# The soft-disc attention layer of a four-layer kernel: steps of a column of four blocks in place of steps of a pair of blocks

## The chip, the core and the metric

The kernel runs on one core of a Trainium2 chip. Its time is device microseconds of one execution, and a version's time is the median over its executions. A core has five engines with a queue of instructions each, worked off in order: TensorE (PE: matrix products, with weight loads of their own, PEld), VectorE (DVE), ScalarE (ACT: functions from tables), GpSimd (POOL) and SyncE (SP: it issues DMAs). [...] Products land in PSUM, which has eight banks of 128 x 512 float32 here.

## What is computed

Four layers work on x, 8 images of 32 x 32 tokens with 256 channels, float32; each adds its result to x after a group normalisation without weights. The first three (retention, an mLSTM, neighbourhood attention) are not touched. The fourth, cut to what matters:

```python
qkv = silu(x @ w_qkv.T)
q, k, v = split(qkv, 3)
q, k = rms_norm(q) * w_qn, rms_norm(k) * w_kn          # per head of 32, 8 heads
wp = silu(x @ w_wp.T + b_wp)
width = sigmoid(wp[..., :8]) * max_dist + 0.5
sharp = sigmoid(wp[..., 8:]) * 9.5 + 0.5
scores = q . k over a 7 x 7 window, * 32 ** -0.5
soft_mask = sigmoid((width - rel_dist) * sharp)
attn = softmax(scores - (1 - soft_mask) * 10000)
out = rms_norm(attn . v over the window) * w_on
x = x + silu((out + v) @ w_out.T)
```

(The reference also rotates q and k, by an angle that depends on the head alone; within a head it is the same for both and cancels in q . k, and the kernel leaves it out, before and after.)

## The kernel before, in words

`layer3` (from line 1991) treats an image's 32 x 32 tokens as a 4 x 4 grid of blocks of 8 x 8. A block's 64 queries see 14 x 14 = 196 keys. Heads come in halves c of four. A *pair* is two blocks under each other in one column (`disc_pairs`, line 1513): 128 queries on the 128 partitions, so an image half has 8 pairs, an image 16, the layer 128 (`st.groups`). For a pair n there are, in order:

- `soft(n)`: four tanh on ACT (line 2133, 128 x 196 each), the soft disc's mask, into one of nine probability tiles `e0` to `e8`; `masked(n)`: one addition on POOL (line 2140, 128 x 784) that shuts out what lies outside the window
- `scores(n)`: 16 products on PE (line 1706) into four PSUM banks, one a head; `logits(n)`: four reductions on DVE (line 1719) that add scores and mask in place and take the row's extremum
- `exps(n)`: four exponentials on ACT (line 1729), which also sum
- `divide(n)`: a reciprocal on DVE (line 1736) and a multiplication on POOL (line 1737)
- `turn(n, i)`: four transposes on PE (line 1747) and a copy on DVE (line 1752), for each i of two
- `values(n)`: products with v on PE (line 1763, 12 in the program, 24 in the trace) and two copies on DVE (line 1771).

All PSUM tiles (four of scores, two of `turn`, one of `values`, and those of the side work) come from one ring of eight banks.

Side work is cut into units that `Fillers` holds with a due time in steps; `units(at)` emits what is due. An image half J (`plan_chunk`) has six projections (`project`, line 2045: two products, a tanh on ACT, line 2042, and a `rest` on DVE and POOL), the sums of squares and their roots (`roots`, line 2144: a table load, a logarithm and an exponential on ACT), four spreading products with scalings of q and k (`head_scale`, line 2171), v laid out in strips on POOL (`in_strips`) and turned on PE (`vturn`). An image (`plan_image`) has its load, statistics, normalisation (`normed`, two on ACT), the disc's parameters (`discs`, line 2083), and its tail: `tail_sq`, `tail_scale`, `reload`, `output` (line 2223). What a unit leaves for DVE and POOL goes to `later`, and `finish()` emits it.

The four compute engines' order is written out by hand: the loop at the end of `layer3` (from line 2347) runs over pairs, and the order in which it calls these functions is the order in each queue. In step n it works on pair n+3 (scores, logits), n+1 (exponentials), n+5 (tanh, mask), n (division), n-2 (turn) and n-3 (values). Every eighth step is `rooted`: there the next half's roots are taken.

Of the kernel before, what the change touches and what calls it, by code (L numbers as in the profile page):

```python
# [1512 lines left out]
def disc_pairs():  # L1513
    return [
        Pair((r, r + 1), c, (8 * r, 8 * r + 8), 8 * c, 14, 14, 0)
        for c in range(4)
        for r in (0, 2)
    ]


# [154 lines left out]
class DiscStream(Stream):  # L1675

# [5 lines left out]
    def __init__(self, K, wk, cp, pp, pairs, n_img, ebufs):  # L1684
        super().__init__(K, wk, pp, pairs, n_img, ebufs)
        self.slots, self.s, self.su = 20, {}, {}
        shape = [P, 4, 2 * self.PART]
        self.tiles = [cp.tile(shape, F32, name=f"e{i}") for i in range(ebufs)]

# [6 lines left out]
    def prob(self, n):  # L1696
        return self.tile(n)[:, :, self.ROW : self.ROW + NWIN]

    def scores(self, n):
        b, c, t = self.groups[n]  # L1700
        s = [self.ring(f"s{j}") for j in range(4)]
        q, k = self.q[b, c], self.k[b, c]
        for g in range(2):
            for j in range(4):
                ch = slice(32 * j, 32 * j + 32)
                self.nc.tensor.matmul(
                    grid(s[j][64 * g : 64 * g + 64, :NWIN], self.ROW),
                    q[ch, 64 * t.block(g) : 64 * t.block(g) + 64],
                    k[ch, t.krs[g] : t.krs[g] + self.ROW, t.kc : t.kc + self.ROW],
                    start=True, stop=True,  # L1710
                )
        self.s[n] = s

    def logits(self, n):

        s, e = self.s.pop(n), self.prob(n)
        self.mx[n] = self.wk.tile([P, 4], F32, name="mx", bufs=self.ebufs)
        for j in range(4):
            self.nc.vector.tensor_tensor_reduce(  # L1719
                e[:, j], in0=s[j][:, :NWIN], in1=e[:, j], scale=MASK_SCALE,  # L1720
                scalar=3.0e38, op0=ALU.add, op1=ALU.min,
                accum_out=self.mx[n][:, j : j + 1],
            )

    def exps(self, n):
        mx, e = self.mx.pop(n), self.prob(n)
        su = self.su[n] = self.wk.tile([P, 4], F32, name="su", bufs=4)
        for j in range(4):
            self.nc.scalar.activation(  # L1729
                e[:, j], e[:, j], AF.Exp, scale=-1.0, bias=mx[:, j : j + 1],  # L1730
                accum_out=su[:, j : j + 1],
            )

    def divide(self, n):
        e, su = self.prob(n), self.su.pop(n)
        self.nc.vector.reciprocal(su, su)  # L1736
        self.nc.gpsimd.tensor_mul(e, e, su.unsqueeze(2).to_broadcast([P, 4, NWIN]))  # L1737

    def turn(self, n, i):

        if i == 0:
            self.pts[n] = self.wk.tile([P, 2, HALF], F32, name="pts", bufs=2)
        ps = self.ring("pt")
        for j in range(2):
            for k in range(2):
                at = (2 * j + k) * P
                self.nc.tensor.transpose(  # L1747
                    ps[: self.PART, at : at + P],
                    self.tile(n)[:, 2 * i + j, k * self.PART : (k + 1) * self.PART],
                    self.K.ident,  # L1750
                )
        self.nc.vector.tensor_copy(self.pts[n][: self.PART, i, :], ps[: self.PART, :])  # L1752

    def values(self, n):
        b, c, t = self.groups[n]
        pts = self.pts.pop(n)
        v, at = self.v[b, c], 5 * t.col + t.rows[0]
        o = self.ring("o")

        for k, q0, o0, w in ((1, 64, 0, P), (0, 0, 64, 64), (2, 192, 0, 64)):  # L1760
            for j in range(4):
                p0 = (j % 2) * 2 * P + q0
                self.nc.tensor.matmul(
                    o[32 * j : 32 * j + 32, o0 : o0 + w],
                    v[: self.PART, at + k, 32 * j : 32 * j + 32],
                    pts[: self.PART, j // 2, p0 : p0 + w],
                    start=k == 1, stop=k != 1, skip_group_check=True,
                )
        for g in range(2):
            d = self.o[b, c][:, t.token(g) : t.token(g) + 1]  # L1770
            self.nc.vector.tensor_copy(
                bass.AP(d.tensor, d.offset, [d.ap[0], [SIDE, 8], [1, 8]]),
                o[:, 64 - 64 * g : 128 - 64 * g].rearrange("p (i j) -> p i j", j=8),
            )
# [216 lines left out]
def layer3(tc, K, src, dst, n_img, a, first):  # L1991
    nc = tc.nc
    pairs = disc_pairs()
    with tc.tile_pool(name="l3c", bufs=1, reuse_waits="tile") as cp, tc.tile_pool(
# [9 lines left out]
        kpad = [cp.tile([P, PADW, PADW], F32, name=f"kp{i}") for i in range(3)]  # L2004
# [3 lines left out]
        st = DiscStream(K, wk, cp, pp, pairs, n_img, 9)  # L2008
        for i in range(3):
            st.clear(i)  # L2010
# [34 lines left out]
        def project(J, s, h):  # L2045
            b, c = divmod(J, 2)
            if h == 0:
                if s == 0:
                    st.q[b, c] = wk.tile([P, L], F32, name="qT", bufs=3)
                elif s == 1:  # L2050
                    st.k[b, c] = kpad[J % 3]
# [76 lines left out]
        def soft(n):  # L2128
            b, c, t = st.groups[n]
            i, e = pairs.index(t), st.prob(n)  # L2130
# [7 lines left out]
        def masked(n):  # L2138
            e = st.prob(n)
            nc.gpsimd.tensor_add(e, e, win[:, 1].unsqueeze(1).to_broadcast([P, 4, NWIN]))  # L2140

        def roots(J, b):
# [19 lines left out]
            n = P if heads else 64  # L2164
# [6 lines left out]
        def head_scale(J, s):  # L2171

            ps = [st.ring("fac_ps") for _ in range(2)]
            for h in range(2):
# [261 lines left out]
```

## Time and profile before

| | |
|---|---|
| median of 3 executions | 3210.92 us (3210.78 to 3218.26) |
| profiled execution | 3219.66 us |
| its span in the profile | 3217.9 us |
| busy, share of the span: PE, DVE, ACT, POOL | 96%, 70%, 68%, 56% |
| the stretch 2500 to 3187 us (soft-disc layer): PE, DVE, ACT, POOL busy | 657.6, 574.3, 580.6, 562.6 of 687 us |
| granted TensorE clock in that stretch | 0.95 |
| first and last reciprocal of line 1736 | 2496.4 and 3183.0 us |

The profile's page cuts the span into 40 slices and gives each engine's busy share in tenths; the last ten are the soft-disc layer. Groups of instructions are given by line, engine, operation and tiles, with their count, busy time, the mean of one and the idle time of the engine ahead of them with what ended it. The ends of PE's products are modelled, so its busy time is an upper bound of its work. The view of the chain that ended last gives nothing here: it holds only the last 5 us.

### The profile page before, as it was taken

To read this page: it belongs to the slowest core of one execution; us is meant where nothing else is said; L and a number is where in the kernel's file an instruction comes from. 1 tells how busy PE (TensorE), PEld (TensorE's weight loads), DVE (VectorE), ACT (ScalarE), POOL (GpSimd) and SP (SyncE) were. 2 spreads that over 40 slices of the span, in tenths; PEclk is the share of its full clock that TensorE was granted. 3 is DMA by queue.
4 is the path that set the end of the run, shared out by engine and by line. 5 is a ranking of instruction groups with operands and counts; after the bars stand their busy time and mean duration, and the time that the engine had idled before them with its cause. 6 is when DMAs were issued, how large, how long until landed. Compare 5 with 4: busy or idle time off the path is not lost. (4 is left out here: it accounts for less than half of the span.)

```text
span 3217.9 us, 76380 instructions
## 1 busy us (share of the span) xinstructions
PE 3096.7 (96%) x30248; PEld 1631.9 (51%) x30248; DVE 2248.8 (70%) x5649; ACT 2186.5 (68%) x4945; POOL 1800.8 (56%) x1201
## 2 busy tenths in 40 slices
PE   7999999999999899999999999999998999999997
PEld 3323223233232444677777766666665555555554
DVE  4786777777776577575666656666665888888885
ACT  3667767776676557655555537667676888888785
POOL 4666666666655111354544545343435778888787
PEclk9999999999999999999999999999998999999998
DMA  3000000000000566888787741111111001111001
GB/s 136 11 27 1 27 27 1 27 21 8 27 14 27 207 242 230 259 224 199 204 229 205 201 153 27 52 68 41 42 52 50 15 15 41 41 41 41 28 28 44
DMA packets 139462, 267.99 MB, mean 83 GB/s; under 512 B 9376, under 2 KB 77984, under 8 KB 130784
## 3 DMA queue, kind: packets, MB, share of 16 engines
q1 hardware_dynamic: 132720, 242.73, 24.7%
q10 hardware_dynamic: 6384, 20.37, 1.9%
q8 instruction: 239, 3.92, 0.5%
q14 instruction: 119, 0.97, 0.1%
HBM read 177.87 MB, written 85.20 MB: 82 GB/s over the span
## 5 line engine op out<-in xcount | busy, mean ns | idle before, releaser
L693 DVE TENSOR_TENSOR e<-s,ret 128x1024 f32<-128x1024 f32 x512 | 602.3, 1218 | 175.8 <-PE s L687 173.3
L700 ACT ACTIVATE ea<-e 128x1024 f32<-128x1024 f32 x512 | 535.4, 1055 | 259.7 <-DVE e L693 237.0
L702 POOL TENSOR_TENSOR ea<-ea 128x1024 f32<-128x1024 f32 x128 | 304.1, 2376 | 288.4 <-ACT ea L700 220.4
L1605 POOL TENSOR_TENSOR e<-e,su 128x616 f32<-128x616 f32 (+2 forms) x128 | 157.3, 1229 | 269.9 <-DVE su L1604 240.2
L687 PE MATMUL s<-qk,qk 32*128 32x512 f32 x2048 | 302.4, 642 | 4.0 <-POOL qk L570 1.8
L739 PE MATMUL num<-e,v 128*32 128x512 f32 x2048 | 272.3, 597 | 0.0
L2133 ACT ACTIVATE e<-win,disc 128x196 f32<-128x196 f32 x512 | 238.9, 540 | 0.2
L1752 DVE COPY pts<-pt 112x512 f32<-112x512 f32 x256 | 174.1, 681 | 86.1 <-PE pt L1747 84.2
L1737 POOL TENSOR_TENSOR e<-e,su 128x784 f32<-128x784 f32 x128 | 191.7, 1497 | 74.6 <-DVE su L1736 37.1
L869 PE MATMUL up_ps<-x,wup 128*128 128x512 f32 x512 | 227.4, 598 | 4.0 <-POOL x L237 3.2
L1729 ACT ACTIVATE e<-e,mx 128x196 f32<-128x196 f32 x512 | 226.8, 447 | 0.0
L2140 POOL TENSOR_TENSOR e<-e,win 128x784 f32<-128x784 f32 x128 | 204.8, 1600 | 26.0 <-ACT e L2133 18.0
L1600 ACT ACTIVATE e<-e,mx 128x154 f32<-128x154 f32 (+2 forms) x512 | 212.3, 426 | 0.0
L712 PE MATMUL sm<-ea,ones 128*32 128x512 f32 x1536 | 209.7, 607 | 1.6 <-POOL ea L702 1.6
L1291 POOL TENSOR_TENSOR decayed<-state,rb 128x520 f32<-128x520 f32 x48 | 50.8, 1057 | 277.9 <-DVE state L1321 161.4
L896 DVE SCALAR_TENSOR_TENSOR cv<-xm,par,cv 128x512 f32<-128x512 f32 x192 | 144.7, 754 | 78.8 <-ACT cv L891 74.2
L2057 PE MATMUL qkv_ps<-xq,w 128*128 128x512 f32 x384 | 195.1, 635 | 4.2 <-DVE v L1785 2.5
L687 PEld LDWEIGHTS s<-qk,qk 32*128 32x128 f32 x2048 | 84.9, 183 | 197.9 <-issue 88.3
L1837 PE MATMUL qkv_ps<-x,w 128*128 128x512 f32 x384 | 183.0, 614 | 1.6 <-POOL x L237 1.6
L1085 ACT ACTIVATE d<-d,cols 128x128 f32<-128x128 f32 x512 | 163.3, 392 | 13.5 <-POOL d L1076 12.9
L1719 DVE CUSTOM_DVE_ANT_0 e<-s,e 128x196 f32<-128x196 f32 x512 | 153.7, 357 | 12.9 <-POOL e L2140 11.2
L1747 PE MATMUL pt<-idg,e 128*112 128x128 f32 x1024 | 157.8, 285 | 4.4 <-POOL e L1737 2.1
(241 smaller groups left out, 6823.1 us busy)
## 6 DMA issues: line engine op xcount, KB each, us to landing
d<-l1rows SPq DMA_DIRECT2D x64, 512.0 KB
x<-x SPq DMA_DIRECT2D x25, 1024.0 KB
l1xm<-xm SPq DMA_DIRECT2D x16, 1024.0 KB
l1sz<-sz SPq DMA_DIRECT2D x16, 1024.0 KB
xv<-l1xm SPq DMA_DIRECT2D x32, 512.0 KB
l1xa<-xa SPq DMA_DIRECT2D x16, 1024.0 KB
xa<-l1xa SPq DMA_DIRECT2D x16, 1024.0 KB
rb<-l1rows SPq DMA_DIRECT2D x32, 512.0 KB
```

The lines of the kernel that those rows point to most:

```text
L687: nc.tensor.matmul(s[:, j % 2], qk[b, 1, c][g, kb * P : (kb + 1) * P], qk[b, 0, c][g, h * HALF : (h + 1) * HALF], start=True, stop=True,)
L693: nc.vector.tensor_mul(e[n, i], s, m)
L700: nc.scalar.activation(ea[n, i], e[n, i], AF.Abs)
L702: nc.gpsimd.tensor_add(ea[n, i], ea[n, i], ea.pop((n - 1, i)))
L712: nc.tensor.matmul(acc["sm"][g, :], ones, two[j // 2][:, j % 2, :], start=kb == 0 and k == 0, stop=kb == 4 and k == 2,)
L739: nc.tensor.matmul(acc["num"][g, :], v[b][:, kb, vc], e[n, j // 2][:, j % 2, :], start=kb == 0, stop=kb == 7,)
L869: nc.tensor.matmul(ps, wup[:, kc, m * P : (m + 1) * P], seg(s)[:, kc], start=kc == 0, stop=kc == 1,)
L1600: self.nc.scalar.activation(p[:, j], p[:, j], AF.Exp, scale=-1.0, bias=mx[:, j : j + 1], accum_out=su[:, j : j + 1],)
L1729: self.nc.scalar.activation(e[:, j], e[:, j], AF.Exp, scale=-1.0, bias=mx[:, j : j + 1], accum_out=su[:, j : j + 1],)
L2057: nc.tensor.matmul(ps, w[:, kc, o : o + P], xq[b][:, kc, h * HALF : (h + 1) * HALF], start=kc == 0, stop=kc == 1,)
L2133: nc.scalar.activation(e[:, j], win[:, 0], AF.Tanh, scale=disc[b][:, i, 8 + h : 9 + h], bias=disc[b][:, i, h : h + 1],)
L2140: nc.gpsimd.tensor_add(e, e, win[:, 1].unsqueeze(1).to_broadcast([P, 4, NWIN]))
```

## The change

Only `DiscStream` and `layer3` are changed. A step now works on a *column* of four blocks, two pairs under each other (g = 0, 1): 64 steps in place of 128.

- Probability tiles are 128 x 2 x 4 x 224, five in place of nine of half the size. A head's scores of both pairs share one bank.
- `logits` takes the heads in two halves, and the division stands between them; one reciprocal serves both pairs.
- `turn(n, j)` handles one head of the column, its four transposes written so that blocks of queries that use the same strip of v lie side by side; `values` has five groups of products in place of twice three, and one copy of 256 columns in place of four of 64.
- Scores run two steps ahead, tanh three, exponentials one, turn one behind and values two behind.
- In a step ACT has the first pair's tanh, the units due, the second pair's tanh, then the exponentials in two parts with units between them. POOL has division and mask ahead of what `finish` brings.
- `roots` is split: the sum of squares is a unit (`squares_sum`), the logarithm and the exponential come at the end of every fourth step, ahead of that step's exponentials.
- The two `head_scale` of a half become one `head_scales`.
- Of q three buffers become two, of the padded k three become two, of the output tile five become four.
- All due times are restated in columns and quarters of a step.

The diff, cut to its core:

```diff
+class DiscStream:
+        shape = [P, 2, 4, 2 * self.PART]
+    def logits(self, n, heads):
+        for j in heads:
+            for g in (1, 0):
+                e = self.prob(n, g)
+                self.nc.vector.tensor_tensor_reduce(
+                    e[:, j], in0=s[j][:, 256 * g : 256 * g + NWIN], in1=e[:, j],
...
+    def turn(self, n, j):
+        d = ps[: self.PART].rearrange("p (g r k x) -> p g k r x", g=2, r=2, k=2)
+        for g in range(2):
             for k in range(2):
                 self.nc.tensor.transpose(
+                    d[:, g, k],
+                    self.tile(n)[:, g, j, k * self.PART : (k + 1) * self.PART],
...
-        for k, q0, o0, w in ((1, 64, 0, P), (0, 0, 64, 64), (2, 192, 0, 64)):
+        for k, m0, o0, w in (
+            (1, 64, 0, P), (3, 320, P, P), (0, 0, 0, 64), (2, 192, 64, P), (4, 448, 192, 64)
+        ):
...
-        for g in range(2):
-            d = self.o[b, c][:, t.token(g) : t.token(g) + 1]
-            self.nc.vector.tensor_copy(
-                bass.AP(d.tensor, d.offset, [d.ap[0], [SIDE, 8], [1, 8]]),
-                o[:, 64 - 64 * g : 128 - 64 * g].rearrange("p (i j) -> p i j", j=8),
-            )
+        self.nc.vector.tensor_copy(
+            grid(self.o[b, c], SIDE)[:, :, 8 * col : 8 * col + 8],
+            o[:, 0:256].rearrange("p (i j) -> p i j", j=8),
+        )
...
-            n, (b, c) = 8 * J, divmod(J, 2)
+            n, (b, c) = 4 * J, divmod(J, 2)
-                fill.add(n - 12 + i / 2, lambda s=s, h=h: project(J, s, h))
-            for s in range(2):
-                fill.add(n - 5 - s, lambda s=s: head_scale(J, s))
-            fill.add(n - 8.5, lambda: project(J, 2, 0))
-            fill.add(n - 8, lambda: project(J, 2, 1))
-            fill.add(n - 6, lambda: in_strips(J))
+                fill.add(n - 6.75 + i // 2 + i % 2 / 4, lambda s=s, h=h: project(J, s, h))
+            fill.add(n - 2.75, lambda: head_scales(J))
+            for h in range(2):
+                fill.add(n - 4.5 + h / 2, lambda h=h: project(J, 2, h))
+            fill.add(n - 2.75, lambda: in_strips(J))
...
-                fill.add(8 * J - 8, lambda J=J, t=t: roots(J, t))
+                fill.add(4 * J - 4.25, lambda J=J, t=t: squares_sum(J, t))
...
-            for n in range(-4, N + 3):
-                if 0 <= n + 3 < N:
...
+            for m in range(-2, N + 2):
+                rooted = m % 4 == 0
+                if m + 2 < N:
+                    st.scores(m + 2)
+                if m + 3 < N:
+                    soft(m + 3, 0)
+                units(m)
+                if m + 2 < N:
+                    st.logits(m + 2, (0, 1))
+                if 0 <= m < N:
+                    st.divide(m)
+                if m + 2 < N:
+                    st.logits(m + 2, (2, 3))
+                if m + 3 < N:
+                    soft(m + 3, 1)
+                    for g in range(2):
+                        masked(m + 3, g)
+                for i in range(2):
+                    if 0 <= m - 1 < N:
+                        st.turn(m - 1, 2 * i)
+                        st.turn(m - 1, 2 * i + 1)
+                    finish()
+                    if not rooted and 0 <= m + 1 < N:
+                        st.exps(m + 1, i)
+                    units(m + 0.25 + i / 4)
+                finish()
                 if rooted:
+                    roots(m // 4 + 1)
+                    if 0 <= m + 1 < N:
+                        st.exps(m + 1, 0)
+                        st.exps(m + 1, 1)
+                if 0 <= m - 2 < N:
...
+                    st.values(m - 2)
+                units(m + 0.75)
```

## The prediction

> **What bounds the kernel now.** I looked first at the busy shares in 40 slices, to find the soft-disc layer (the last quarter, from 2443 us to the end at 3217.9), then at the start times of the reciprocal of line 1736, one a pair of blocks: image by image its first one stands at 2496.4, 2580.0, 2673.2, 2761.7, 2853.8, 2946.6, 3040.8 and 3126.3 us, so an image with all its side work takes 83.6 to 94.2 us. Two such images, engine by engine (us, busy, granted clock, DMA):
>
> ```profile
> 2678.60:2770.50 91.90, 89.85 (x1002) 51.44 (x1001) 78.23 (x286) 79.57 (x230) 76.50 (x56) 0.98 0.11 36
> 2770.50:2862.40 91.90, 88.54 (x953) 50.88 (x952) 76.84 (x277) 75.97 (x221) 74.94 (x56) 0.94 0.11 36
> ```
>
> The order is PE, weight loads, DVE, ACT, POOL. PE is within 2 to 3 us of full (its ends are modelled), the other three stand 12 to 17 us below the period. Who waits for whom between 2500 and 3187 us, in us, times, longest:
>
> ```profile
> DVE pts L1752 <- PE pt L1747: 84.2, 81, 2.5
> ACT th L2042 <- PE qkv_ps L2057: 69.1, 33, 6.2
> ...
> ACT th L2042 <- PE out_ps L2227: 29.3, 27, 2.3
> POOL e L1737 <- ACT fac L2168: 29.3, 6, 5.6
> POOL e L1737 <- DVE su L1736: 29.1, 20, 3.5
> ```
>
> ACT's idle time is 106 of 687 us, and 98 of it is two waits for PE: the tanh of a projection (L2042) that PE has not finished. DVE's largest wait is for PE too. So PE sets the pace in the steps that project, ACT in those that take roots or have no side work. What one image holds (form, count, busy us, mean ns, idle before):
>
> ```profile
> L2133 ACT ACTIVATE e<-win,disc 128x196 f32<-128x196 f32 x64 | 29.9, 540 | 0.0
> L1729 ACT ACTIVATE e<-e,mx 128x196 f32<-128x196 f32 x64 | 28.4, 447 | 0.0
> L1737 POOL TENSOR_TENSOR e<-e,su 128x784 f32<-128x784 f32 x16 | 23.9, 1497 | 8.7 <-ACT fac L2168 4.9 <-DVE su L1736 3.7
> L1752 DVE COPY pts<-pt 112x512 f32<-112x512 f32 x32 | 21.8, 682 | 12.7 <-PE pt L1747 12.4
> ...
> L1771 DVE COPY oT<-o 128x64 f32<-128x64 f32 x32 | 5.5, 215 | 0.0
> ```
>
> **A measure of the old order.** From the timeline of 2770 to 2862 us, from one start to the next, PE takes 0.52 us for a pair's scores, 0.44 for four transposes, 0.58 for a pair's values (2.0 a pair in all), 1.8 for a projection, 1.75 for an output product, 1.85 for two spreading products of the roots, 1.9 for half an image's disc product, 1.05 for a tail product, 0.45 for a turn of v, 0.9 for the squares' sum (2.7 with the tail's). ACT takes 1.77 for four tanh or four exponentials (3.55 a pair), 0.55 for a projection's tanh, 1.23 for a normed half, 1.28 for a table load, 0.6 each for logarithm and exponential of the roots. Put in the sixteen steps of an image where the code has them, that makes 82.2 us for PE and 76.1 for ACT. The larger of the two, step by step, is 6.6, 7.3, 3.85, 7.65, 5.6, 5.6, 3.55, 4.7, 6.6, 4.85, 3.85, 5.1, 6.65, 7.35, 4.65, 8.2: together 92.1 us, against 91.9 of the window. So the old loop behaves nearly as if no step could lend time to the next, and I use the same measure on the new one.
>
> **The change, part by part.** *Fewer instructions.* Four copies of 64 columns a column of blocks become one of 256: the four take 4 x 0.175 us from start to start (two show as 0.35 in the timeline), the one, between 0.175 at 64 and 0.68 at 512 columns, 0.39; 0.31 saved, 2.5 us an image. One reciprocal instead of two saves some 0.08, 0.7 an image. Both are on DVE, which idles 15 us an image; I count them at nothing, and 3.2 us an image where DVE turns out to bound. Value products go from 24 to 20 a column with the same columns streamed; between nothing and 4/24 of 1.16 us, 0 to 1.5 us an image on PE; I take 0.5, near the columns' answer. Banks of PSUM fall from 19.3 to 14.3 a column, so scores wait less for a bank; the waits of L1706 are under 2 us an image now, so nothing. Tanh, exponentials, divisions, masks, table loads and DMAs keep their number (division and mask 1.5 and 1.6 us each on POOL). Loads and reloads are issued at the same place of the stream to within half a column; POOL has waited 0.7 us in all for them, so nothing while SP has slack.
>
> *The tanh of a projection moves.* It stood right behind four exponentials; now it stands behind two groups of tanh and one of exponentials (5.3 us), the second one behind 7.1. This answers the 98 us of waits: 13 us an image.
>
> *Steps become lumpy.* Eight steps an image, in each PE's 4.0 us and ACT's 7.1 plus the side work of the new schedule (two spreading pairs, two projections and half a disc product in step 1; two projections, half a disc product and two turns of v in 2; one projection, two turns, the squares in 3; one projection and the roots in 4; spreading, projections and two tail products in 5; two projections and an output in 6; one projection and two outputs in 7; projection, output, normed halves, roots in 0):
> PE 8.0, 13.1, 10.4, 9.4, 6.2, 13.3, 10.5, 11.3 = 82.2; ACT 13.1, 9.7, 8.7, 7.9, 10.1, 9.5, 8.75, 8.75 = 76.5. The larger each time: 13.1, 13.1, 10.4, 9.4, 10.1, 13.3, 10.5, 11.3 = 91.2 us. By this measure the change gives 0.9 us an image: the heavy PE steps stand where ACT is light and the reverse, in both orders.
>
> *What is added.* The last projection, v's second half, comes first in steps 0 and 4, and its tanh stands behind one group of tanh only. By the changed program's listing its bank is that of a tile which DVE empties after ACT's last tanh of the step before: two half copies of 0.42 and in step 0 an output's 0.68. So PE starts it 0.8 to 1.5 us into ACT's step, ends at 2.6 to 3.3, and ACT needs it at 1.77: 0.8 to 1.5 us, and another 1.2 for the output behind it in step 0. DVE may be later than that: in step 5 four scalings of q and k (2.6), two tail scalings (3.0), statistics (1.5) and the projections stand behind 5.6 us of fixed work, 4 us more than ACT's step. Then the logits of step 6 are late by these 4 us, the banks of the second projection with them, and ACT waits 1 to 2 us in steps 6 and 7. In steps 2 and 3 the disc's three scalings do the same; there POOL is busy, and these small instructions stretch (ns, least, median, longest):
>
> ```profile
> L2124 DVE SCALAR_TENSOR_TENSOR disc<-disc x16: 192/1158/1509, 2460.4 to 3067.5; 128x32 f32<-128x32 f32 x16
> ```
>
> Behind them are v's copies, and behind those PE's next projection. In all 2 to 6 us of new waits an image; the old order has its like (the two longest waits for a projection are 4.1 and 4.3 us in the second window), but there they are in the 92.1. I take 3, nearer the lower end since the longer cover repays a part: 91.2 - 0.5 + 3 = 93.7, 1.8 more than 91.9. Over seven images with side work: 12.6. Before the first reciprocal the same tanh and exponentials stand in ACT's queue; nothing. At the end the last column needs one more division (1.5) and two more copies (1.4) than the last pair: 3. Sum: 15.6, say 16.
>
> *The clock.* In the second window PE twice ran at less than full clock:
>
> ```profile
> 2789.00:2799.00 10.00, 7.64 (x90) 5.34 (x92) 9.11 (x32) 5.89 (x19) 8.29 (x7) 0.83 0.01 2
> ...
> 2814.00:2824.00 10.00, 9.66 (x63) 4.61 (x61) 8.17 (x34) 5.74 (x22) 8.23 (x7) 0.66 0.01 2
> ```
>
> By the granted share 10 x 0.17 and 10 x 0.34 us of PE's work are lost, 5 us an image. I leave this as it is: by the sums above PE idles some 9 us an image in the new order too, in pieces of a microsecond or two. [...]
>
> **Rivals.** (1) *The longer cover wins.* If steps lend time to each other, PE alone is the bound: 82.2 - 0.5, the 5 of the clock, and 1 to 2 of gaps, 88 to 89 us an image; 3 to 4 less than now, seven times 25, less the end's 3: 3189, and down to 3175 if two of the clock's 5 us go as well. For it: all 98 us of ACT's waits are at the moved instruction, and its cover grows from 1.77 to 5.3 us and more. Against: the measure above says that it was not order inside a step. (2) *A wash*: new waits of 0 to 2 us, 91 to 92 us an image: 3205 to 3218. (3) *POOL becomes the bound* on the slower side: in step 5 it has 6.2 us of divisions and masks, 5.1 of tail adds, 2.1 of squares and 1.75 of strips, 15.2 against ACT's 9.5, and no slack until step 0; the masks of step 6 would then end 4 us into step 7 and the output's add, whose tile one of three th buffers is, behind them. It decides once POOL is over 5 us late, and costs 3 to 5 us more an image: 3250 to 3262. It is the upper end of the likeliest case.
>
> **How the numbers follow.** The times stand against the profiled execution's own 3219.66 us (span 3217.9 and 1.8 around it), which is 8.7 above the median of 3210.92; I put the difference on the median: 3210.9 + 15.6 = 3227. A change under 0.3% (9.6 us) can't be told from none. Chances: slower by waits of DVE and the lumps 0.42, by POOL 0.09 (0.51 slower); a wash 0.14; faster by cover 0.35. The likeliest one's own range is 3221 to 3262; with the others, 3175 to 3262.
>
> **What would show it.** Right, if the idle time of ACT moves from the waits for projections at the steps' ends to the first projection of steps 0 and 4, each 2 to 5 us, DVE's wait for transposes stays over 50 us, and an image takes 93 to 95 us. Wrong, if ACT's waits for L2042's successor fall below 50 us over the layer and an image takes under 90; or if the granted clock rises to 1.0 there. POOL's case shows as DVE's logits waiting for masks.

## The result, and the profile after

| | before | after |
|---|---|---|
| median of 8 executions each, us | 3210.09 (3193.61 to 3218.26) | 3231.07 (3227.61 to 3240.39) |
| ratio, after to before | | 1.0072, 95% interval 1.0052 to 1.0091 |
| span of the profiled execution, us | 3217.9 | 3229.5 |
| layer: first reciprocal at, us | 2496.4 | 2489.7 |
| seven images, from first to first reciprocal, us | 629.9 | 641.4 |
| from the last image's first reciprocal to the end, us | 91.6 | 98.5 |

The changed kernel is slower by 0.5 to 0.9%. The two profiled executions are 11.6 us apart, the medians 21: the profiled execution of before took 3219.66 us, 9.6 above its median, that of after 3231.35. So the traces can place 11.6 us, and they place them thus: 6.7 less up to the first reciprocal, 11.5 more in the seven images, 6.9 more from there to the end.

The first view is that of stretches, two whole images of the changed kernel (us; then PE, weight loads, DVE, ACT, POOL busy; granted clock, DMA):

```profile
2665.40:2758.30 92.90, 81.71 (x889) 50.48 (x888) 75.91 (x246) 76.41 (x222) 73.95 (x55) 0.94 0.11 34
2758.30:2851.60 93.30, 82.52 (x889) 50.68 (x888) 75.85 (x248) 76.52 (x222) 73.95 (x55) 0.95 0.12 36
```

Each engine's work is what it was or less, PE's by 6 to 7 us (its ends are modelled, so that a part of this is no work), and an image takes 1 to 1.4 us longer. Who waits for whom between 2500 and 3187 us (in us, times, longest):

```profile
POOL e L1740 <- DVE su L1737: 106.8, 40, 6.7
...
DVE pts L1757 <- PE pt L1752: 58.9, 21, 8.6
ACT th L2044 <- PE qkv_ps L2059: 44.5, 25, 2.8
DVE su L1737 <- ACT e L1730: 41.7, 14, 5.3
...
ACT disc L2117 <- DVE disc L2112: 24.0, 7, 3.8
...
ACT th L2044 <- PE out_ps L2236: 19.7, 17, 1.6
```

ACT's waits for projections and outputs fell from 98 to 64 us. New ones came: the reciprocal waits for the exponentials, ACT for DVE's small operations on the disc, and POOL waits most of all, so over the whole stretch it is not the bound. The second image step by step, each step from its reciprocal to the next (same columns):

```profile
2758.30:2772.40 14.10, 10.24 (x114) 6.19 (x112) 7.34 (x30) 11.46 (x27) 7.29 (x5) 0.87 0.57 173
2772.40:2786.80 14.40, 13.15 (x115) 8.77 (x116) 8.96 (x30) 11.50 (x34) 9.83 (x8) 0.77 0.01 4
2786.80:2799.10 12.30, 10.51 (x130) 7.91 (x129) 12.27 (x32) 12.03 (x41) 11.70 (x9) 1.00 0.01 3
2799.10:2808.50 9.40, 8.95 (x104) 4.17 (x103) 9.37 (x33) 4.27 (x14) 6.01 (x4) 1.00 0.01 2
2808.50:2817.30 8.80, 7.97 (x109) 5.62 (x107) 7.73 (x31) 8.54 (x25) 6.01 (x4) 1.00 0.01 2
2817.30:2831.60 14.30, 11.70 (x104) 5.76 (x104) 12.86 (x38) 14.29 (x42) 13.18 (x11) 1.00 0.00 0
2831.60:2840.80 9.20, 9.20 (x110) 6.14 (x109) 8.81 (x34) 6.91 (x20) 9.20 (x8) 1.00 0.01 3
2840.80:2851.60 10.80, 10.80 (x113) 6.10 (x112) 8.52 (x32) 7.53 (x25) 10.72 (x9) 1.00 0.21 68
```

This is the table that the rest rests on. Look in each row for an engine whose busy time is the length of the step: from step 2 on there is one in every row: DVE in steps 2 and 3, ACT in 4 (nearly) and 5, PE in 6 and 7, where POOL is full as well. Only steps 0 and 1, the two behind the roots, have slack on every engine (11.46 of 14.10 and 13.15 of 14.40), and PE's 13.15 there is at a granted clock of 0.77. Over the whole image no engine is above 82.5 of 93.3 us; in its own step one of them nearly always is full.

Two cautions belong to this table. The first: busy is not the same as at work. In steps 2 and 3 DVE is held up inside small operations on the disc's parameters. In step 2 of the image that begins at 2665.4 us there are five (start, us, engine, line):

```profile
2695.04 1.39 DVE L2112 SCALAR_TENSOR_TENSOR disc<-dth,disc 128x64 f32<-128x64 f32 x1
...
2698.15 0.21 DVE L2099 TENSOR_TENSOR disc<-wp_ps,bwp 128x64 f32<-128x64 f32 x1
...
2698.88 0.41 DVE L2124 TENSOR_SCALAR disc<-disc 128x32 f32<-128x32 f32 x1
...
2699.21 1.62 DVE L2125 TENSOR_SCALAR disc<-disc 128x32 f32<-128x32 f32 x1
...
2700.86 1.50 DVE L2126 SCALAR_TENSOR_TENSOR disc<-disc 128x32 f32<-128x32 f32 x1
```

They take 5.1 us; the shortest that each of them takes in the traces of the changed kernel and of e2_disc adds up to 1.0 us. So DVE was occupied throughout the step, with some 8 us of work in 12.3. The second: a row is cut at DVE's reciprocals, and ACT's queue does not keep to them. A column alone has 24 ACT instructions (8 tanh, 8 exponentials, 8 reads of their sums); row 3 shows 14 in all, row 5 shows 42. So a row can be set beside the program's sum for that step only roughly.

### The profile page after: what moved, and what is told of

Read it like the earlier page. It is cut to its first block, busy times and chain, and to the rows that moved or that the text cites. A ratio compares the mean times of both kernels' runs of the same rounds, so it can differ in the third digit from the quotient of the medians.

```text
span 3229.5 us, 74992 instructions
## 1 busy us (share of the span) xinstructions
PE 3046.0 (94%) x29736; PEld 1626.0 (50%) x29736; DVE 2239.0 (69%) x5393; ACT 2187.6 (68%) x4945; POOL 1792.5 (56%) x1196
## 5 line engine op out<-in xcount | busy, mean ns | idle before, releaser
L2059 PE MATMUL qkv_ps<-xq,w 128*128 128x512 f32 x384 | 204.3, 661 | 37.1 <-DVE mx L1719 21.9
L1757 DVE COPY pts<-pt 112x512 f32<-112x512 f32 x256 | 163.1, 683 | 66.4 <-PE pt L1752 66.2
L1752 PE MATMUL pt<-idg,e 128*112 128x128 f32 x1024 | 143.2, 281 | 26.2 <-DVE qT L2069 10.7
L1719 DVE CUSTOM_DVE_ANT_0 e<-s,e 128x196 f32<-128x196 f32 x512 | 150.8, 351 | 20.7 <-PE s L1703 10.1
```

The lines of the kernel that those rows point to most:

```text
L2059: nc.tensor.matmul(ps, w[:, kc, o : o + P], xq[b][:, kc, h * HALF : (h + 1) * HALF], start=kc == 0, stop=kc == 1,)
```

## The experiments

Each kernel is an edit of the changed kernel or of one that stands above it. The ratio is to the kernel before, run beside each of them (its medians lie between 3207.9 and 3213.0 us), with the 95% interval. "Seven images" and "end" are the two stretches of the table above, from one profiled execution each; e3_v1 and e6_drain, alike up to the end, agree in them to 0.1 us an image, e8_lump and e10_best to 1.7, and the start (2487 to 2494 us in all these kernels) differs by 1 to 3 us in both pairs.

| kernel | edit | median, us | ratio | seven images | end |
|---|---|---|---|---|---|
| after | | 3231.07 | 1.0072 (1.0052 to 1.0091) | 641.4 | 98.5 |
| e1_recip | reciprocal behind all logits | 3228.45 | 1.0071 (1.0054 to 1.0089) | 640.4 | 99.8 |
| e2_disc | disc's functions later | 3229.68 | 1.0084 (1.0065 to 1.0103) | 641.2 | 98.5 |
| e3_v1 | v's second projection later | 3219.45 | 1.0043 (1.0030 to 1.0056) | 629.2 | 100.2 |
| e4_k0 | k's first projection ahead of the spreading | 3236.34 | 1.0091 (1.0077 to 1.0106) | 647.7 | 99.3 |
| e6_drain | e3, tail of image 6 later | 3215.63 | 1.0015 (1.0003 to 1.0027) | 629.1 | 95.2 |
| e7_cover | kernel before, tanh ahead of the units | 3221.41 | 1.0030 (1.0019 to 1.0041) | 641.2 | 88.3 |
| e8_lump | e3, two projections a step earlier | 3201.16 | 0.9971 (0.9958 to 0.9984) | 610.5 | 97.8 |
| e9_waits | e1 + e2 + e3 | 3230.10 | 1.0068 (1.0049 to 1.0087) | 632.5 | 98.7 |
| e10_best | e8 + e6's edit | 3196.57 | 0.9956 (0.9941 to 0.9970) | 609.4 | 93.4 |
| e11_disc2 | e10 + e2's edit | 3196.13 | 0.9954 (0.9940 to 0.9968) | 608.9 | 95.0 |
| e12_pool | after, division and mask behind the leftovers | 3350.86 | 1.0434 (1.0415 to 1.0453) | 760.7 | 98.7 |
| e13_recip2 | e10 + e1's edit | 3203.32 | 0.9972 (0.9960 to 0.9984) | 613.5 | 95.5 |

The steps of an image (mean of the five images from the second to the sixth, us from reciprocal to reciprocal), worked out from the same traces; before, such an image took 92.2 us:

| step | 0 | 1 | 2 | 3 | 4 | 5 | 6 | 7 | sum |
|---|---|---|---|---|---|---|---|---|---|
| prediction's sums | 13.1 | 13.1 | 10.4 | 9.4 | 10.1 | 13.3 | 10.5 | 11.3 | 91.2 |
| after | 13.7 | 13.9 | 12.3 | 9.5 | 9.1 | 14.6 | 9.5 | 10.8 | 93.4 |
| e1_recip | 12.5 | 12.7 | 12.2 | 10.2 | 8.6 | 15.0 | 9.6 | 10.8 | 91.7 |
| e2_disc | 13.7 | 13.7 | 10.8 | 10.2 | 9.5 | 15.4 | 9.5 | 10.8 | 93.6 |
| e3_v1 | 12.1 | 13.9 | 12.3 | 9.4 | 8.1 | 14.7 | 10.9 | 10.9 | 92.2 |
| e4_k0 | 13.7 | 13.8 | 11.4 | 9.3 | 8.9 | 15.8 | 10.2 | 10.8 | 93.9 |
| e8_lump | 12.1 | 12.2 | 12.6 | 9.3 | 9.2 | 12.8 | 9.8 | 10.5 | 88.6 |
| e9_waits | 11.0 | 12.7 | 10.4 | 10.3 | 9.4 | 17.3 | 9.9 | 10.9 | 91.8 |
| e10_best | 12.1 | 12.1 | 12.7 | 9.4 | 9.3 | 12.8 | 9.7 | 10.6 | 88.6 |
| e13_recip2 | 11.0 | 10.3 | 13.4 | 10.3 | 9.2 | 12.8 | 10.9 | 10.8 | 88.6 |

### Four waits taken away, one at a time

**e1_recip**

```diff
-                    st.logits(m + 2, (0, 1))
+                    st.logits(m + 2, (0, 1, 2, 3))
                 if 0 <= m < N:
                     st.divide(m)
-                if m + 2 < N:
-                    st.logits(m + 2, (2, 3))
```

> Edit of the changed kernel: all eight logits of a column stand ahead of its reciprocal, where four stood behind it. Theory A (the slow-down is made of waits that the new order makes; here DVE holds the banks of two heads while it waits for ACT's exponentials, 5.3 us of wait in the step after the roots, once in four steps, and the wait of DVE's reciprocal for ACT's exponentials is 41.7 us in all): the PE wait for the banks (2.1 us a time, two an image) goes, 13 to 22 us less than the changed kernel's 3231, so 3209 to 3218. Rival (the wait is hidden, or POOL, which now gets its division later, passes the delay on): within 10 us of 3231, or slower, with the wait of POOL's division for the reciprocal growing from 106.8 us.

The wait fell (41.7 to 24.3 us), POOL's wait for the reciprocal grew (106.8 to 122.7), and the ratio is that of the changed kernel, the last two as the rival said. But the steps did not give everything back: steps 0 and 1 are 1.1 and 1.2 us shorter, step 3 is 0.7 and step 5 0.4 longer, and each of the five middle images keeps 1.7 us. What takes these 8.7 us away again in the trace stands elsewhere: the first of the seven images and the last are each 4 us longer (87.0 and 95.2 against 82.9 and 91.5) and the end 1.3; the first reciprocal comes 2.6 earlier. In the last image it is step 5, which takes 18.3 us, 12.7 of them with PE at half clock (13.5 us and no half clock in the changed kernel). The steps with slack became shorter, as theory A said, and the kernel did not; why the first image became longer was not tried.

**e2_disc**

```diff
             def silu2(th):
...
-                return sigmoid
+                return lambda: sigmoid
```

(and the same one function earlier, for `silu`)

> Edit of the changed kernel: the two later functions that ACT takes for the disc's parameters (a silu and a sigmoid, both by tanh) are put off by one turn of the list of leftovers, so that they stand behind the next group of exponentials and not ahead of it. Theory A: the waits of ACT for DVE's small disc operations (24.0 + 8.0 us between 2500 and 3187, longest 3.8) go from ACT, and 10 to 25 us of the 32 from the time: 3206 to 3221. Rival (PE is the bound in those steps and lends the time away): the waits go and the time stays within 5 us of 3231, while the waits of ACT for projections grow by as much.

The rival, in every point that it named. Between 2500 and 3187 us:

```profile
ACT th L2044 <- PE qkv_ps L2059: 80.5, 35, 5.4
```

ACT's waits for the disc are gone, those for projections are 36 us longer (44.5 before the edit). In the table, step 2 becomes 1.5 us shorter, and steps 3, 4 and 5 take back 0.7, 0.4 and 0.8. DVE's hold-up moved with the edit: its operations on the disc took 5.1, 2.6 and 0 us in steps 2, 3 and 4 (mean of the five images), and now take 0.7, 3.5 and 1.9. So a DVE without slack in step 2 cannot be why the time stayed: it is now busy there for 8.1 of 10.8 us. What the hold-up itself costs was not tried apart.

**e3_v1**

```diff
-                fill.add(n - 4.5 + h / 2, lambda h=h: project(J, 2, h))
+                fill.add(n - 4.5 + h * 0.75, lambda h=h: project(J, 2, h))
...
-                fill.add(n + (14.5, 15.25, 15.5, 16)[i], lambda h=h, m=m: output(b, m, h))
+                fill.add(n + (14.5, 15.25, 15.5, 16.25)[i], lambda h=h, m=m: output(b, m, h))
```

> Edit of the changed kernel: the second projection of v stands a quarter of a step later (behind the second tanh group and the first exponentials of steps 0 and 4, not first in them), and the last output a quarter later too. This is the step of the prediction that takes 0.8 to 1.5 us of ACT wait in steps 0 and 4 and 1.2 for the output behind it. Theory A (as the prediction): the tanh's waits at the head of steps 0 and 4 (2.7 + 1.1 and 1.9 us in one image) go, 20 to 35 us less than 3231: 3196 to 3211. Rival (these steps are bound by PE, and the later place only moves the wait): within 10 us of 3231.

Steps 0 and 4 are 1.6 and 1.0 us shorter, step 6 1.3 longer; all seven images together 12.2 us. That is the whole excess of the changed kernel in the images: 629.2 against 629.9 before. By the ratios it is 0.0029 of 3210, 9 us: less than the theory's 20, and by the medians (11.6 us) just more than the rival's 10, so it falls between the two. It is the only one of the four edits that pays, and it acts in step 0, where no engine was full. It moves two things, v's projection and the last output, which were not tried apart.

**e4_k0**

```diff
-                fill.add(n - 6.75 + i // 2 + i % 2 / 4, lambda s=s, h=h: project(J, s, h))
+                fill.add(n - 6.75 - 0.01 * (i == 0) + i // 2 + i % 2 / 4, lambda s=s, h=h: project(J, s, h))
```

> Edit of the changed kernel: in the step after the roots the first projection of k is emitted ahead of the four spreading products and scalings, not behind them. Theory A: PE has a projection to do while it waits for the roots (the wait of PE and of its weight loads for the roots' factors, 14.5 and 16.0 us over six visible times, 2.4 to 2.7 us each) and does not fall to half clock behind it (10.2 us at half clock in one place, 92 us in the layer): 10 to 20 us less than 3231, with less time at half clock. Rival (the wait is that of the roots themselves on ACT, and the scalings then come later to scores that need them): within 10 us or slower, with the half clock as before.

The rival, on its slower side: step 1 keeps its 13.8 us, step 5 grows by 1.2. PE's wait for the roots fell from 14.5 to 4.2 us, but its wait for DVE's logits, which stood ahead of the projections (21.9 us), now stands ahead of the spreading products (21.8), and the half clock cost 40.0 us where it had cost 42.2. Filling the wait with work of the same step gained nothing.

### Two theories of a step's length

What remains is between two readings: that the position of an instruction inside its step matters (rival 1 of the prediction and my theory A), or that each step has its own load, and only moving load between steps helps (the prediction's measure).

**e7_cover** (edit of the kernel before)

```diff
-                if rooted and 1 < n + 5 < N:
+                if 1 < n + 5 < N:
                     soft(n + 5)
                 units(n)
...
-                if not rooted and 1 < n + 5 < N:
-                    soft(n + 5)
```

> Edit of the kernel before: the four tanh of the soft disc stand ahead of the step's units in every step, not only in every eighth, and nothing else changes (steps of a pair, divisions and masks as they were). This is the part of the change that the prediction's first rival lives by. Rival (the longer cover wins): the 98 us of ACT's waits for projections and outputs fall under 50 and the time by 10 to 25 us: 3185 to 3200. The prediction's measure (each step costs the larger of PE's and ACT's work, and the order inside it is worth little): waits fall, the time stays within 10 us of 3208.

It is slower by 0.3% (9.6 us by the ratio, just inside the 10 us of the prediction's measure) and 11.3 us longer in the seven images. Neither side was right about the waits between 2500 and 3187 us:

```profile
ACT th L2042 <- PE qkv_ps L2057: 78.4, 46, 6.2
...
ACT th L2042 <- PE out_ps L2227: 17.3, 20, 1.5
```

They are 96 us against 98: a cover of 3.5 us in place of 1.8 does not take the waits away, it moves them. (That the four tanh are missing behind the first projection, where the next one's tanh now waits, is my reading; it was not tried apart.) The images grow by 11.3 us here and by 11.5 in the whole change. So the earlier tanh alone costs, in the old order, all that the images lost, and e3_v1 wins as much back by moving v's projection and an output: which of the two parts is the cause in the new order is not shown.

**e8_lump** (e3_v1, and this)

```diff
-                fill.add(n - 6.75 + i // 2 + i % 2 / 4, lambda s=s, h=h: project(J, s, h))
+                fill.add(n - 6.75 + i // 2 + i % 2 / 4 - (0.5 + i / 4) * (i < 2 and J > 2), lambda s=s, h=h: project(J, s, h))
```

> Edit of the kernel e3_v1: the first two projections of each half (from the third on) stand at the end of the step before, where ACT is the longer engine by the prediction's sums (13.1 against PE's 8.0 us in step 0, 10.1 against 6.2 in step 4), and no longer in steps 1 and 5, where PE is (13.1 and 13.3 us). By the prediction's measure steps 1 and 5 lose 3.6 us each, steps 0 and 4 gain 1.1 each: 5 us an image, six images, 30 us: 3189, and the steps after the roots shrink from 13.9 and 14.7 us to about 11. Rival (steps lend each other time, so that PE's work counts wherever it stands): within 8 us of 3219.

Faster than the kernel before. Steps 1 and 5 become 1.7 and 1.9 us shorter (3.6 expected), step 6 another 1.1, step 0 stays and step 4 grows by 1.1: 3.7 an image, 18.7 over the seven, where 30 were worked out. The first two rows of an image of e3_v1, then the first, second and sixth of one of e8_lump:

```profile
2756.80:2769.10 12.30, 9.30 (x108) 5.61 (x106) 7.30 (x30) 9.60 (x24) 7.28 (x5) 0.97 0.57 171
2769.10:2783.20 14.10, 12.88 (x115) 8.51 (x116) 8.98 (x30) 11.51 (x33) 9.86 (x8) 0.79 0.07 21
```

```profile
2750.50:2762.80 12.30, 12.30 (x112) 6.83 (x110) 7.41 (x30) 9.59 (x24) 8.08 (x6) 1.00 0.62 185
2762.80:2774.90 12.10, 9.70 (x111) 7.58 (x111) 9.11 (x32) 11.05 (x32) 10.53 (x9) 0.86 0.10 31
...
2806.00:2818.80 12.80, 10.90 (x103) 6.42 (x102) 12.77 (x40) 12.79 (x40) 12.43 (x11) 0.87 0.00 1
```

In step 0 of e3_v1 PE had 9.30 of 12.30 us, and now it has 12.30 of 12.30. Step 5 does not come down to 11, which fits that DVE and ACT are busy throughout it and POOL nearly so. A projection moved within its step (e4_k0) was worth nothing; two moved over the step's border are worth 23 us by the ratios (0.0072 of 3210).

### Do the waits count once the load is levelled?

**e9_waits** (e1, e2 and e3 together) and, on the levelled kernel, **e11_disc2** (e10 with e2's edit) and **e13_recip2** (e10 with e1's):

> Edit of the kernel e3_v1 with the two edits of e1_recip and e2_disc, which gave 3 and 1 us alone. Theory (the waits that they remove were hidden because another engine came last in the same steps, and still does): within 5 us of 3219. Rival (v's projection was what hid them, so that now they count): 10 to 25 us less, 3194 to 3209.

> e10_best with the edit of e2_disc (disc's second and third functions behind the next exponentials). With the projections moved, step 2 is among the longest that are left (12.6 us from reciprocal to reciprocal, against 10.4 of PE's work by the prediction's sums). Theory (what is won in one step is given back in the next ones, in waits of ACT for projections and in time at half clock, as in e2_disc and e9_waits): within 5 us of e10_best. Rival (with the load levelled, ACT's waits for the disc are on the path now): 8 to 15 us less, step 2 at about 11 us.

> e10_best with the edit of e1_recip (all eight logits ahead of the reciprocal). In e1_recip steps 0 and 1 became 1.1 and 1.2 us shorter and step 3 and the last image longer, and the time stayed. Theory (given back elsewhere, as in e1_recip, e9_waits and e11_disc2): within 5 us of 3196.6. Rival (steps 0 and 1, 12.1 us each, are now among the longest and nothing takes the gain back): 7 to 16 us less, 3181 to 3190.

None gained. e9_waits is 8 us slower than e3_v1 by the ratios (their intervals touch), which neither side expected. In its trace steps 0 to 2 become 4.2 us shorter, steps 3, 4 and 5 take back 4.8, 2.6 of it in step 5, and step 6 is 1.0 shorter. So the five middle images keep 0.4 us each; the first image is 4.4 longer. The execution profiled is the fastest of six (3222.31 us), so the trace does not hold the 8 us. e11_disc2 is e10_best's equal. In e13_recip2 steps 0 and 1 become 2.8 us shorter, steps 2, 3 and 6 together 2.7 longer, and the sum is 88.6 for both. Its median is 7 us worse (5 by the ratios, whose intervals overlap); in the trace that is the first image, 4.1 us longer as in e1_recip and e9_waits, and 2 us each at the start and the end. PE had less time at half clock in it, too: 24.6 us of its work lost in 687, by the stretches for which the profile records a halved clock, against 35.8 in e10_best. That did not make it faster.

So the measure does not hold step by step: e13_recip2 has 11.0 us between the marks of step 0, where the prediction's sum for ACT is 13.1, so a part of that step's work stands beyond its marks. What the runs support is weaker: load moved between steps shortened the middle images more (3.7 us each, e8_lump) than any edit of the order inside steps (1.7 at most, e1_recip).

### The end, and GpSimd's order

**e6_drain** (e3_v1, and this; `b == n_img - 2` is image 6)

```diff
-                fill.add(n + 13.25 + c / 4, lambda c=c: tail_scale(2 * b + 4, b, c))
+                fill.add(n + 13.25 + 3 * (b == n_img - 2) + c / 4, lambda c=c: tail_scale(2 * b + 4, b, c))
...
+                late = (3.75, 3.25, 4.5, 4)[i] if b == n_img - 2 else 0
-                fill.add(n + (14.5, 15.25, 15.5, 16.25)[i], lambda h=h, m=m: output(b, m, h))
+                fill.add(n + (14.5, 15.25, 15.5, 16.25)[i] + late, lambda h=h, m=m: output(b, m, h))
```

(the last reload of that image moves with them)

> Edit of the kernel e3_v1 (v's second projection later): the scalings and additions of image 6's tail, and its outputs, are moved by three to four steps, behind the last two divisions. Theory: the 8.5 us that the changed kernel takes longer from its last reciprocal to the end (43.4 against 34.9; e3_v1: 46.1) are the five us of POOL's tail additions that stand ahead of the last two divisions, and what follows from them; with them behind, 5 to 9 us less than e3_v1's 3219, so 3210 to 3214, and no slower than before. Rival (the end is bound by PE, or by the squares and roots of the last image): within 3 us of e3_v1.

What it acts on stands in the timeline of the changed kernel (start, us, engine, line):

```profile
3180.59 4.99 POOL L2228 TENSOR_TENSOR oT<-oT,vT 128x512 f32<-128x512 f32 x4 [1.12 <-DVE oT L2225]
...
3182.74 0.20 DVE L1737 RECIPROCAL su<-su 128x8 f32<-128x8 f32 x1
...
3185.53 2.95 POOL L1740 TENSOR_TENSOR e<-e,su 128x784 f32<-128x784 f32 x2
...
3186.12 0.20 DVE L1737 RECIPROCAL su<-su 128x8 f32<-128x8 f32 x1
...
3188.43 1.28 POOL L2245 TENSOR_TENSOR xr<-xr,th 128x512 f32<-128x512 f32 x1
...
3189.66 2.95 POOL L1740 TENSOR_TENSOR e<-e,su 128x784 f32<-128x784 f32 x2
```

The division of the last column but one waits 2.8 us behind image 6's tail additions (its reciprocal is at 3182.74); that of the last one starts 3.5 us after its reciprocal, behind this division and an output's addition. With the tail behind them the end is 5.0 us shorter than e3_v1's (95.2 against 100.2), the ratio falls by 0.0028, 9 us, the upper end of what was expected. The other two forecasts were just missed: the median of 3215.63 stands above 3210 to 3214 (the kernel before took 3211.91 beside it, and 3207.90 beside e3_v1), and the kernel is still 0.15% slower than before, with an interval of 0.03 to 0.27%.

**e10_best** (e8_lump with e6's edit)

> The edits of e8_lump and e6_drain together on the changed kernel. They touch different stretches (the steps after the roots; what follows the last division), so they should add: e8_lump's 3201 less the 4 to 9 us that e6_drain gained on e3_v1: 3192 to 3197, faster than both kernels. If the two are not independent (the tail of image 6 is cover for PE in the last image), 3201 or more.

As expected, and faster than both kernels: 0.44% under the kernel before. Of the 5 us by which its median is under e8_lump's the intervals leave open whether it is 0 or 10.

**e12_pool**: the one part undone, POOL's priority over what the side units leave to it (the leftovers, which `finish` emits).

```diff
-                    for g in range(2):
-                        masked(m + 3, g)
                 for i in range(2):
...
                     finish()
+                    if i == 0 and 0 <= m < N:
+                        st.multiply(m, su)
...
                 finish()
+                for g in range(2 if m + 3 < N else 0):
+                    masked(m + 3, g)
```

(`divide` keeps the reciprocal where it was; `multiply` is its product on POOL)

> Edit of the changed kernel that undoes one part of it: GpSimd's division stands behind the first lot of leftovers of its step and the masks behind all of them, as they did before the change. Theory (GpSimd has slack: it idles 145 of 687 us and waits 106.8 us for the reciprocal, and its place in the order hardly counts): within 8 us of 3231. Rival (that part is worth something, because transposes wait for the division and the next logits for the mask): 15 to 40 us slower, with the waits of transposes for the division and of DVE's logits for the mask above all others.

Both were wrong, mine altogether: 120 us slower, three times the rival's upper end. The waits (this kernel's L2145 is the mask, L1743 the division):

```profile
DVE e L1719 <- POOL e L2145: 162.1, 38, 6.0
POOL e L1743 <- DVE su L1737: 91.2, 40, 5.9
```

POOL still waits 91 us for the reciprocal, and DVE waits 162 us for the masks; in the changed kernel that was 9.9. (PE's transposes wait only 10.7 us for the division, so that half of the rival's sign did not come.) A column's mask, made at the end of a step, is wanted by the logits at the head of the next. Steps 1 and 5 take 20.7 and 20.8 us. PE also lost 77 us of its work to the half clock between 2500 and 3187, where the changed kernel lost 42; how much of the 120 us that is was not tried. An engine with a fifth of its time idle can still set the end through the place of its instructions: here one division and two masks a step, moved together. (In the kernel before the mask stands as far down its step, but two steps ahead of its logits; so this run prices the part in the new order, not in the old.)

## Why the prediction was right, point by point

- **The forecast.** 3227 was forecast, 3231 measured, for nearly the reasons given: the images, 12.6 us more by the prediction and 11.5 in the trace; the end, 3 and 6.9; the start, 0 and 6.7 less. That 3227 and 3231 are so close is in part luck. Trace against trace the change is 11.6 us, where the sum said 15.6: the start and the end are missed by 6.7 and 3.9 us, in opposite directions. Of the medians, which are 21 us apart, some 9 us belong to no stretch that I can name, since the profiled execution of before was longer than its median by as much. And the images did not grow by 1.8 us each: the seven changed by -0.7, -0.4, 4.4, 1.2, -0.1, 1.1 and 6.0 us, so nearly all of it is in the third and the last. In just these two the kernel before had lost little to the half clock (1.7 and 0.0 us), and the changed one lost 3.4 us more in each. What was named as a sign came: ACT's idle time at the first projection of steps 0 and 4 (2.7 + 1.1 us in step 0 and 1.9, just under the 2 that were named, in step 4 of the second image), DVE's wait for transposes over 50 us (58.9), an image of 93 to 95 us (92.7 to 95.3 from the second to the sixth).
- **The measure** (each step costs the larger of PE's and ACT's work, no step lends time). Upheld in the main: other positions inside a step gained the kernel nothing (e1, e2, e4, e7), but for v's projection in a step with slack (e3), and load moved over a border is worth most of what the sums say (e8_lump, 3.7 us an image of 5). Not upheld in its strict form: e1_recip shortened the middle images by 1.7 us each with order alone, and ACT's work runs over the borders of the steps. A further fault is that it has two engines of four. DVE is occupied throughout steps 2 and 3, held up for a third of step 2; POOL is busy throughout 6 and 7, and in 5 DVE and POOL are nearly as busy as ACT. Step 2 was put at 10.4 and took 12.3, step 5 at 13.3 and took 14.6. That this made the gain expected of e8_lump too large is likely, not shown.
- **The moved tanh** was said to answer 98 us of waits, 13 an image, and stands in the sum at nothing. The waits fell to 64 us, and the time did not follow; e7_cover shows that the longer cover alone gains nothing; in the old order it costs 11.3 us in the images. So rival 1 falls, and even a price of nothing may have been too low.
- **v's second projection first in steps 0 and 4**: 0.8 to 1.5 us of wait in each, 1.2 more for the output, taken with the rest as 3 us an image. The waits were there and larger (2.7 and 1.9 us in the second image, 1.1 for the output), and e3_v1 prices the step: 12.2 us of 641.4, all that the images had grown. That this step is what made them grow does not follow, since the moved tanh costs as much by e7_cover.
- **DVE late in step 5, hence waits of ACT in 6 and 7**: ACT did wait there, 2.3 us in step 6 and 1.2 in step 7 of the second image, but mostly for PE's outputs, and the steps took 9.5 and 10.8 us, less than their sums. **The disc's small operations in steps 2 and 3** were late as foreseen, but ACT waited for them (24.0 us), not PE behind v's copies; and e2_disc shows that without this wait the time is the same, while DVE's hold-up moves on to steps 3 and 4.
- **The end** was mis-sized. One more division and two more copies were 3 us; it left out that image 6's tail stands on POOL ahead of the last two divisions (e6_drain gives back 5.0).
- **The clock** was to stay at 5 us an image. From its record 42.2 us were lost between 2500 and 3187, 34.1 before: 1.1 us an image more. In the images it falls where the growth is, but it does not set the time by itself: e3_v1 lost 44.4 us and its images are 12.2 us shorter, and e13_recip2 lost 24.6 without being faster. What part it has in the slow-down stays open.
- **Rival 3** (POOL the bound) did not come about. e12_pool shows that POOL can hold up the kernel all the same: not by its sum of work but by its order.

That the start became shorter is not explained for certain. e7_cover, with the tanh ahead in the old order, shows 5.3 of the 6.7 us (2491.1), so the earlier tanh is the likely cause; it was not tried by itself in the new order.

## What to carry to other kernels

Cut the loop at a repeating mark and look, stretch by stretch, for an engine that is busy throughout: with such an engine in nearly every stretch, a wait of another engine can be taken away without any gain, though its sum in the list of waits is tens of microseconds. Then move work over the border to a stretch where its engine has slack, which here gained 0.7% with one line, while of five edits of order inside the steps four gained nothing and one 0.3%. Count all engines in each stretch, and before you call one full, compare its instructions with their own shortest durations: it may be held up inside them (five on the disc here took 5.1 us, their shortest 1.0). Keep what the next step needs first in the queue of an engine that serves several masters.

## What the runs showed of the hardware

In the changed kernel's record of the clock between 2443 and 3187 us, PE's clock is at 0.50 for fifteen stretches of 3.41, 6.83, 10.24 or 13.65 us, all multiples of 3.41, and the longest gap between PE's products in the 6.9 us ahead of each is between 0.8 and 3.1 us; in the kernel before it is 0.34 us ahead of one of 6.83 us, from 2816.0 on. A gap of 2.42 us (waiting for the roots) stands ahead of this one of the changed kernel:

```profile
2768.80:2779.00 10.20, 7.96 (x23) 4.36 (x24) 2.48 (x11) 10.17 (x34) 6.02 (x4) 0.50 0.33 115
```

In e9_waits PE was idle for 1.45 of the 6.8 us ahead, the longest gap was 1.41 us, in step 4, and the half clock runs on into step 5:

```profile
2800.40:2807.20 6.80, 5.35 (x92) 3.61 (x90) 6.73 (x15) 6.72 (x21) 6.02 (x4) 1.00 0.00 0
2807.20:2814.00 6.80, 6.80 (x11) 2.66 (x10) 4.42 (x22) 6.57 (x17) 3.99 (x3) 0.50 0.01 2
```

By the granted share 6.8 us at 0.50 hold 3.4 us of work; a projection's four products take 3.75 us at half clock in the changed kernel (from 2773.30 us) and 1.88 at full (from 2785.83). Over the five middle images step 5 of e9_waits lost 2.7 us to the half clock, that of e3_v1 0.8, which is most of the 2.6 us that it grew by; that it is the cause is not shown. In e10_best step 5 takes 12.8 to 12.9 us whether 0 or 3.4 us are lost in it.

A DVE operation of 128 x 64 took 215 ns in the kernel before and up to 1397 in the changed one (ns: least, median, longest):

```profile
L2110 DVE SCALAR_TENSOR_TENSOR disc<-dth,disc x16: 214/215/356, 2458.9 to 3060.3; 128x64 f32<-128x64 f32 x16
```

```profile
L2112 DVE SCALAR_TENSOR_TENSOR disc<-dth,disc x16: 219/975/1397, 2452.6 to 3082.1; 128x64 f32<-128x64 f32 x16
```

In the changed kernel's trace the 14 long ones (0.97 to 1.40 us) end 80 to 86 ns after a POOL instruction that was already running when they began. The kernel before has it too, in other operations on the disc (13 of L2124's, 0.91 to 1.51 us, end 46 to 53 ns after such an instruction): together they take 6.0 us of DVE an image there, 8.0 in the changed kernel and 6.3 in e2_disc (mean of the five middle images), where the operation shown has a median of 219 ns. What this costs the kernel is not shown: e2_disc takes away 1.7 us an image of it and moves the rest, and the time is the same.
